# Turning two of four attention heads with VectorE and a trip through DRAM instead of TensorE

## The chip, the cores and the metric

The kernel runs on one core of a Trainium2 chip. A core has five engines that run their own instruction streams side by side and wait for each other by semaphores: TensorE (PE in the profile; PEld is its weight load) multiplies matrices into PSUM, VectorE (DVE) and ScalarE (ACT) work elementwise and along rows, GpSimd (POOL) helps, and SyncE (SP) here issues nearly all DMAs. The metric is the device time of one execution in microseconds. Before the change the median of three runs is 820.45 us (820.26 to 821.07).

## The reference

For 16 batches of 128 rows and 1024 columns: a layer norm, grouped-query cross attention to a context (32 query heads of size 32, 8 key/value heads, four query heads to a key head), a residual, a second layer norm, a product with a 0/1 matrix whose last fifth of the rows counts as -4, a scale and a second residual.

```python
Q = query @ Wq + bq
K = key @ Wk + bk
V = value @ Wv + bv
...
scores = jnp.einsum('bhgqd,bhkd->bhgqk', Q, K) * scale
w = jax.nn.softmax(scores, axis=-1)
y = jnp.einsum('bhgqk,bhkd->bhgqd', w, V)
...
x = x + _L0_xattn_ref(_layernorm(x, axis=-1), ctx_4096, ctx_4096, ...)
x = x + _L0_ffn_ref(_layernorm(x, axis=-1), L0_ffn_kernel, L0_ffn_scale)
```

## The kernel before, in words

All data are float32. The 16 batches go in eight **groups** of two (`grp` 0 to 7). The attention of a group falls into four **steps**: for each of the two chunks `a` of four key heads, the two batches. A step (`attend`, L669, then `weighted`, L551) works as follows.

- `scores` (L506): 16 groups of matmuls of 32 rows write, for each key head `i` of the chunk, a PSUM tile of 128 query positions by 4 query heads by 128 key positions.
- `exponentials` (L522), for each of the four key heads: VectorE takes the negative maximum (`negm`, L525), ScalarE writes `p`, the exponential, once for each query head with its sum (L529).
- `divide` (L538): VectorE takes the reciprocal (L540) and multiplies `p` in place (L541).
- `turn` (L543): TensorE transposes the four 128x128 blocks of `p` against the identity (`tpp`, L546), as the sum over key positions needs the key position in the partitions; ScalarE copies the result from PSUM to SBUF (`pt`, L548).
- `weighted` (L551): four matmuls of 512 columns with `v` as weights (`av`, L556), and a copy to `yT` (L564).

The score tiles, `p` and `pt` each have four buffers, one to a key head.

Between these the other work of the group is woven in: the query projection (`prep_q`, L430; matmuls at L396) and output projection (`out_proj`, L568; L607), each made of seven products instead of eight with sums of blocks (`seven`, L407) whose weights do not fit and are streamed from DRAM in **pieces** of 512 KB through a ring of eight (`fetch`, L213, issued on SP at L218), the key and value projections (`accumulate`, L293), and the second product (`ffn`, L652, also L293) with its transposes (`ffn_transpose`, L636). `norm_x` (L335) normalizes the next group's `x` on VectorE, and `prep_x` (L329) transposes it on TensorE (`tp_x`, L310). The next context is loaded by eight 128 KB DMAs a group, each to 32 partitions (`load_ctx`, L151, issued at L156); VectorE turns it in blocks of 32x32 (`turn_ctx`, L314, L319). The output is stored at L667.

The order is written out by hand by `Stream` (L23). It has a queue of generators, each of which emits a piece of TensorE work and yields its cost in microseconds, and a list of events with due times. `run` (L52) fires each event whose due time has passed, then emits the next piece and adds its cost to the clock. An event may add a cost too (0.45 for a `turn`). So an event lands at the first boundary between pieces after its due time; a piece of the output projection costs 2 x 512/600 = 1.71, one of the query projection 2 x 128/600 = 0.43. Instructions of each engine run in the order in which they are emitted here.

A step starts with the scores (1.2 on the clock). `first` for key head `i` is due 0.7 + 2.4 i after that, `divide` 2.3 after `first`, and the turn `length`/2 - 3.0 after `first` (L681 to L687). Other work is then emitted until `length` - 2.0 after the step's start (L872), in the last step of a group until the queue is empty (L870), and then until all four heads are turned (L873). Then comes `weighted`. `length` (L815) is 17.4 in group 0, 24.0 in groups 1 to 5 and 22.0 in group 6; group 7 has its own rule (L857 to L864).

Of the kernel before, what the change touches and what calls it, by code (L numbers as in the profile page):

```python
# [9 lines left out]
FP = mybir.dt.float32  # L10
# [7 lines left out]
P = 128  # L18
# [58 lines left out]
def once(fn, *args):  # L77
    fn(*args)
    yield 0.0
# [3 lines left out]
def kernel(  # L83
# [16 lines left out]
    nc = tc.nc  # L100
    B, S, D = x.shape
    KV = Wk.shape[1]
    F = ffn_w.shape[1]
    HD = 32
    NG = D // KV
    NI = P // HD
# [11 lines left out]
    const = ctx.enter_context(tc.tile_pool(name="const", bufs=1))  # L118
    dram = ctx.enter_context(tc.tile_pool(name="dram", bufs=1, space=bass.MemoryType.DRAM))
    work = ctx.enter_context(tc.tile_pool(name="work", bufs=1))  # L120
    small = ctx.enter_context(tc.tile_pool(name="small", bufs=4))
    ps_mm = ctx.enter_context(tc.tile_pool(name="ps_mm", bufs=2, space=PSUM))
    ps_tp = ctx.enter_context(tc.tile_pool(name="ps_tp", bufs=2, space=PSUM))
    ps_sc = ctx.enter_context(tc.tile_pool(name="ps_sc", bufs=4, space=PSUM))

    ident = const.tile([P, P], FP, name="ident")
# [214 lines left out]
    def prep_k(grp):  # L341
        kT = work.tile([P, NA, T], FP, tag="kT", name=f"kT{grp}", bufs=2)
        kTs[grp] = kT
        for a in range(NA):
            mm = ps_mm.tile([P, T], FP, tag="mm", name=f"k_{grp}_{a}")
            yield from accumulate(
                mm, [(wk_sb[:, c, a * P : (a + 1) * P], chunk(cTs, grp, c)) for c in range(NC)]
            )
            nc.scalar.activation(kT[:, a], mm, AF.Identity, bias=bkT[:, a : a + 1])
            yield 0.85  # L350
# [13 lines left out]
    S4 = [P, NG, S]  # L364
# [139 lines left out]
    yTs = {}  # L504

    def scores(b, a):  # L506
        grp, cols = b // GB, slice(b % GB * S, (b % GB + 1) * S)
        qT, kT = qTs[b, a], kTs[grp]
        tiles = [ps_sc.tile([P, NG, S], FP, tag="sc", name=f"sc_{b}_{a}_{i}") for i in range(NI)]
        for g in range(NG):  # L510
            for i in range(NI):
                rows = slice(i * HD, (i + 1) * HD)
                nc.tensor.matmul(  # L513
                    tiles[i][:, g],
                    lhsT=qT[rows, g],
                    rhs=kT[rows, a, cols],
                    start=True,
                    stop=True,
                )
        return tiles  # L520

    def exponentials(b, a, i, tile_):  # L522
        n = f"{b}_{a}_{i}"
        negm = small.tile([P, NG], FP, tag="negm", name=f"negm_{n}")
        nc.vector.tensor_reduce(negm, tile_, AX.X, ALU.max, negate=True)  # L525
        p = work.tile([P, NG, S], FP, tag="p", name=f"p_{n}", bufs=4)
        total = small.tile([P, NG], FP, tag="total", name=f"total_{n}")
        for g in range(NG):
            nc.scalar.activation(  # L529
                p[:, g],  # L530
                tile_[:, g],
                AF.Exp,
                bias=negm[:, g : g + 1],
                accum_out=total[:, g : g + 1],
            )
        return p, total

    def divide(b, a, i, p, total):  # L538
        inv = small.tile([P, NG], FP, tag="inv", name=f"inv_{b}_{a}_{i}")
        nc.vector.reciprocal(inv, total)  # L540
        nc.vector.tensor_mul(p, p, inv.unsqueeze(2).to_broadcast([P, NG, S]))  # L541

    def turn(b, a, i, p):  # L543
        tp = ps_tp.tile([P, NG, S], FP, tag="tp", name=f"tpp_{b}_{a}_{i}")
        for g in range(NG):
            nc.tensor.transpose(tp[:, g], p[:, g], ident)  # L546
        pt = work.tile([P, NG, S], FP, tag="pt", name=f"pt_{b}_{a}_{i}", bufs=4)
        nc.scalar.copy(pt, tp)  # L548
        return pt

    def weighted(b, a, pts):  # L551

        mm = ps_tp.tile([P, NG, S], FP, tag="tp", name=f"av_{b}_{a}")
        for i in range(NI):
            h = a * NI + i
            nc.tensor.matmul(  # L556
                mm[i * HD : (i + 1) * HD],
                lhsT=vs[b][:, h * HD : (h + 1) * HD],
                rhs=pts[i],
                start=True,  # L560
                stop=True,
            )
        yTs[b, a] = work.tile(S4, FP, tag="yT", name=f"yT{b}_{a}", bufs=7)
        nc.scalar.copy(yTs[b, a], mm)  # L564

    x2Ts, x2ns, x2stats = {}, {}, {}

# [98 lines left out]
        if b < B - 1:  # L666
            nc.sync.dma_start(out=out[b], in_=x_t)  # L667

    def attend(b, a, length):  # L669


        tiles = scores(b, a)
        stream.now += 1.2
        pts = [None] * NI
        for i in range(NI):

            def first(i=i):
                p, total = exponentials(b, a, i, tiles[i])
                stream.later(2.3, lambda: divide(b, a, i, p, total))

                def third():  # L681
                    pts[i] = turn(b, a, i, p)
                    return 0.45

                stream.later(length / 2 - 3.0, third)

            stream.later(0.7 + 2.4 * i, first)  # L687
        return pts

    def combine(w, k, part):  # L690

# [44 lines left out]
    NGRP = B // GB  # L736
    with tc.manual_schedule():
        stream = Stream()
# [15 lines left out]
        def plain(a):  # L754
            return prep_q_plain(a, {(r, k): at_q[r, a, k] for r in range(2) for k in range(2)})
# [47 lines left out]
        def between(gen, n, fn, *args):  # L803

            for i, us in enumerate(gen):
                yield us
                if i + 1 == n:
                    fn(*args)

        for grp in range(NGRP):  # L810
            b0, b1, nxt = grp * GB, grp * GB + 1, grp + 1
            p0, p1 = b0 - 2, b0 - 1
            first, more = grp == 0, nxt < NGRP
            last = grp == NGRP - 1
            length = 17.4 if first else 24.0 if grp < NGRP - 2 else 22.0  # L815
            if first:
                stream.add(
                    once(prep_ctx, nxt, 12.5, 13.5),
                    between(plain(1), 9, sums_of_wq, 0),
                    once(sums_of_wq, 1),  # L820
                    once(turn_ctx, nxt * GB, 1),
                    once(turn_ctx, nxt * GB + 1, 1),
                    once(norm_x, nxt * GB),
                    prep_k(nxt),
                    once(get_ctx, nxt + 1),
                    once(norm_x, nxt * GB + 1),
                    prep_v(nxt),
                    prep_x(nxt, 0),
                    prep_x(nxt, 1),
                    once(convert_ffn),  # L830
                    between(qs[nxt], 40, residuals, grp),
                )
            elif more:
                stream.add(
                    once(get_x, nxt * GB, 14.0),
                    once(prep_ctx, nxt, 3.7, 8.0, 13.0, 18.0),
                    os[grp - 1],
                    once(get_ctx, nxt + 1),
                    prep_k(nxt),
                    mixed(prep_v(nxt), chain(ffn_transpose(p0), ffn_transpose(p1)), 1, 2),  # L840
                    once(get_x, nxt * GB + 1, 5.0),
                )
                if nxt < NGRP - 1:
                    stream.add(ffn(p0), mixed(ffn(p1), prep_x(nxt, 0), 12))
                else:
                    stream.add(mixed(ffn(p0), prep_x(nxt, 0), 14))
                stream.add(once(residuals, grp), prep_x(nxt, 1), qs[nxt])
            else:
                stream.add(
                    os[grp - 1],  # L850
                    mixed(ffn(p1 - 2), ffn_transpose(p0), 10, 2),
                    once(load_residual, b0, 2.0),
                    mixed(ffn(p0), ffn_transpose(p1), 8, 2),
                    once(load_residual, b1, 2.0),
                )
            if not more:
                for q in range(2 * NA):  # L857
                    b, a = grp * GB + q % GB, q // GB
                    start = stream.now
                    pts = attend(b, a, 15.0)  # L860
                    stream.later(15.0, lambda b=b, a=a, pts=pts: weighted(b, a, pts) or 1.0)
                    stream.run(start + 12.0)
                stream.drain()
                break  # L864
            for q in range(2 * NA):
                b, a = grp * GB + q % GB, q // GB
                start = stream.now
                pts = attend(b, a, length)
                if q == 2 * NA - 1:
                    stream.run(start + length - 2.0, lambda: stream.queue)  # L870
                else:
                    stream.run(start + length - 2.0)  # L872
                stream.run(stream.now, lambda: None in pts)  # L873
                weighted(b, a, pts)
                stream.now += 1.0
        stream.add(
            os[NGRP - 1],
# [54 lines left out]
```

## Time and profile before

| what | value |
|---|---|
| median of three runs | 820.45 us |
| the profiled execution, and its span | 817.83 us, 816.1 us |
| one of groups 1 to 5 | 97.5 to 97.6 us |
| group 6, group 7 | 92.5 us, 110.8 us |
| transposes of `p` on TensorE (L546) | 512, mean 273 ns |
| copies of them on ScalarE (L548) | 128, mean 590 ns |
| block transposes of the context on VectorE (L319) | 32, mean 698 ns |
| pieces of weights | 218 DMAs of 512 KB, 4.4 to 4.8 us to land (medians by source) |
| DMA over the span | 165.14 MB, 202 GB/s |

The profile shows one execution. A group of instructions is named by its line in the kernel, its engine and what it writes and reads. A mean duration is that of one instruction from its start to its modelled end, and matmuls overlap; the chain of work that ended last gives each piece of work only the time by which it put off what came after. The span is the profiled time from first to last instruction. A DMA has an issue on SP's queue (SPq) and a landing. Where the text gives an instruction's time, it is from the span's start; where it gives a time within a step, it is from the step's first score matmul.

### The profile page before, as it was taken

The page shows a single profiled execution, that of the slowest core. Times are in us where ns is not written, and L with a number is a line of the kernel's source. Part 1 is how long each engine was busy: PE and PEld are TensorE (multiplying, and loading weights), DVE is VectorE, ACT ScalarE, POOL GpSimd, SP SyncE. Part 2 cuts the span into 40 slices and gives each one's busy share as a digit, 9 for nine tenths or more (in the row PEclk, how much of TensorE's full clock was granted, in tenths as well). Part 3 has the DMA queues.
Part 4 walks back from the last instruction along what each step waited for, and adds up shares of the span by engine and source line. Part 5 has one row for each costly group of instructions (what it writes and reads, how often), then busy time and mean ns, then how long its engine had stood idle before and what let it go on. Part 6 is the DMA issues. An engine that isn't in the chain of part 4 may idle for free.

```text
span 816.1 us, 13885 instructions
## 1 busy us (share of the span) xinstructions
PE 789.8 (97%) x5216; PEld 593.4 (73%) x5216; DVE 459.9 (56%) x862; ACT 332.7 (41%) x1281; POOL 69.6 (9%) x109
## 2 busy tenths in 40 slices
PE   3997999999999999999999999999999999999998
PEld 3886884678947797488965889568894779756556
DVE  1369748554475554755456454765348565467442
ACT  0243854444334443345333544344434454366200
POOL 1000003002000020000300002000200002000300
PEclk9999999999999999999999999999999999999999
DMA  9999598715885178741887328780578307761511
GB/s 202 357 319 317 198 399 326 210 52 182 273 269 164 43 238 274 262 130 44 286 269 253 80 103 280 276 242 29 179 262 281 132 27 274 246 215 69 195 62 77
DMA packets 81075, 165.14 MB, mean 202 GB/s; under 512 B 5969, under 2 KB 42833, under 8 KB 81009
## 3 DMA queue, kind: packets, MB, share of 16 engines
q1 hardware_dynamic: 79200, 162.55, 59.6%
q10 hardware_dynamic: 1664, 1.57, 1.1%
q8 instruction: 41, 0.67, 0.3%
q0 software_dynamic: 144, 0.14, 0.1%
q14 instruction: 26, 0.20, 0.1%
HBM read 147.46 MB, written 16.78 MB: 201 GB/s over the span
## 4 chain that ended last, share of the span: by engine, by line
PE 86%; DMA 6%; DVE 3%; issue 2%; SPq 1%; ACT 1%; POOL 0%; ACTq 0%; DVEq 0%; POOLq 0%
PE o_u L607 14%; PE f L293 14%; PE q_u L396 12%; PE o_v L607 7%; PE tpp L546 6%; PE q_v L396 6%; PE k L293 5%; PE v L293 5%; PE sc L513 4%; PE av L556 4%; PE o_c L607 3%; PE q_c L396 3%; DMA wo<-in_L_xattn_Wo_dram 2%; PE tp_f L646 2%; PE tp_x L310 1%
## 5 line engine op out<-in xcount | busy, mean ns | idle before, releaser
L529 ACT ACTIVATE p<-sc,negm 128x128 f32<-128x128 f32 x512 | 181.1, 369 | 155.9 <-DVE negm L525 82.3
L548 ACT COPY pt<-tpp 128x512 f32<-128x512 f32 x128 | 74.8, 590 | 117.1 <-PE tpp L546 116.6
L525 DVE TENSOR_REDUCE negm<-sc 128x4 f32<-128x512 f32 x128 | 87.3, 683 | 39.8 <-PE sc L513 39.8
L293 PE MATMUL f<-wf_sb,x2l 128*128 128x512 f32 x256 | 106.0, 414 | 0.0
L529 ACT ACTIVATION_READ_ACCUMULATOR p<-sc,negm 128x1 f32 x512 | 105.8, 207 | 0.0
L293 PE MATMUL f<-wf_sb,x2h 128*128 128x512 f32 x256 | 101.2, 396 | 0.0
L541 DVE TENSOR_TENSOR p<-p,inv 128x512 f32<-128x512 f32 x128 | 88.6, 692 | 4.4
L546 PE MATMUL tpp<-ident,p 128*128 128x128 f32 x512 | 76.7, 273 | 6.3 <-DVE p L541 4.0
L546 PEld LDWEIGHTS tpp<-ident,p 128*128 128x128 f32 x512 | 61.7, 141 | 28.1 <-issue 20.0
L396 PE MATMUL q_u<-t,piece 128*128 128x128 f32 x672 | 81.2, 276 | 0.0
L396 PEld LDWEIGHTS q_u<-t,piece 128*128 128x128 f32 x672 | 78.0, 192 | 0.2 <-DMA piece<-q 0.2
L293 PE MATMUL v<-wv_sb,cT 128*128 128x256 f32 x256 | 62.6, 387 | 12.3 <-DMA wv_sb<-in_L_xattn_Wv_dram 12.3
L178 POOL TENSOR_TENSOR x<-x,bo_b 128x256 f32<-128x256 f32 x64 | 48.8, 795 | 180.2 <-DMA x<-in_x_dram 160.1
L293 PEld LDWEIGHTS v<-wv_sb,cT 128*128 128x128 f32 x256 | 47.5, 195 | 17.7 <-issue 12.3
L607 PE MATMUL o_u<-piece,yT 128*128 128x512 f32 x128 | 59.1, 603 | 0.0
L607 PE MATMUL o_u<-piece,s 128*128 128x512 f32 x128 | 59.0, 594 | 0.0
L607 PE MATMUL o_v<-piece,s 128*128 128x512 f32 x128 | 59.0, 594 | 0.0
L293 PE MATMUL k<-cT,wk_sb 128*128 128x256 f32 x256 | 57.0, 380 | 0.0
L293 PEld LDWEIGHTS f<-wf_sb,x2l 128*128 128x128 f32 x256 | 48.1, 188 | 11.4 <-issue 1.1
L293 PEld LDWEIGHTS f<-wf_sb,x2h 128*128 128x128 f32 x256 | 48.3, 189 | 10.0 <-issue 0.5
L293 PEld LDWEIGHTS k<-cT,wk_sb 128*128 128x128 f32 x256 | 48.5, 190 | 9.0 <-issue 2.6
L564 ACT COPY yT<-av 128x512 f32<-128x512 f32 x32 | 18.7, 585 | 88.0 <-PE av L556 88.0
(77 smaller groups left out, 949.8 us busy)
## 6 DMA issues: line engine op xcount, KB each, us to landing
piece<-o SPq DMA_DIRECT2D x64, 512.0 KB, 4.4
piece<-q SPq DMA_DIRECT2D x56, 512.0 KB, 4.4
piece<-in_L_xattn_Wq_dram SPq DMA_DIRECT2D x50, 512.0 KB, 4.8
piece<-in_L_xattn_Wo_dram SPq DMA_DIRECT2D x48, 512.0 KB, 4.5
xn<-in_x_dram SPq DMA_DIRECT2D x16, 512.0 KB, 5.4
x<-in_x_dram SPq DMA_DIRECT2D x16, 512.0 KB, 4.9
ctx<-in_ctx_dram SPq DMA_DIRECT2D x60, 128.0 KB, 5.9
out_dram<-x SPq DMA_DIRECT2D x15, 512.0 KB, 2.7
```

Source lines behind the costliest of these rows:

```text
L178: lambda cut=cut: nc.gpsimd.tensor_add(x_t[:, cut], x_t[:, cut], bo_b[:, cut]) and None,
L293: nc.tensor.matmul(mm, lhsT=lhsT, rhs=rhs, start=k == 0, stop=k == n - 1)
L396: nc.tensor.matmul(mm if part is None else mm[:, part], lhsT=lhsT, rhs=rhs, start=start and n == k == 0, stop=k == len(some) - 1, skip_gro ...
L513: nc.tensor.matmul(tiles[i][:, g], lhsT=qT[rows, g], rhs=kT[rows, a, cols], start=True, stop=True,)
L525: nc.vector.tensor_reduce(negm, tile_, AX.X, ALU.max, negate=True)
L529: nc.scalar.activation(p[:, g], tile_[:, g], AF.Exp, bias=negm[:, g : g + 1], accum_out=total[:, g : g + 1],)
L541: nc.vector.tensor_mul(p, p, inv.unsqueeze(2).to_broadcast([P, NG, S]))
L546: nc.tensor.transpose(tp[:, g], p[:, g], ident)
L548: nc.scalar.copy(pt, tp)
L556: nc.tensor.matmul(mm[i * HD : (i + 1) * HD], lhsT=vs[b][:, h * HD : (h + 1) * HD], rhs=pts[i], start=True, stop=True,)
L564: nc.scalar.copy(yTs[b, a], mm)
L607: nc.tensor.matmul(mm, lhsT=lhsT[:, 2 * k + c], rhs=w[:, c], start=start and k == c == 0, stop=k == c == 1, skip_group_check=True,)
```

## The change

In groups 1 to 6, the first two of a step's four key heads are no longer transposed by TensorE. VectorE transposes their scaled `p` in place, in blocks of 32x32 (`turn_blocks`). What is left is to move whole blocks between quarters of the partitions: SP stores both heads to DRAM in one DMA (`store_blocks`), and fetches them back in four DMAs of 128 KB, one to each quarter of 32 partitions (`fetch_blocks`). For this the exponentials of the two heads are written in blocks of 32 key positions, the two heads side by side, so that a block row of both is 1 KB. `p` and `pt` become two constant tiles of four heads each, `p_all` and `pT_all`, in place of four rotating buffers each. The turned `p` of all heads lies with the query block outermost, and the weighted sum reads four runs of 128 columns and is put in order by the copy to `yT`. The other two heads, and all heads of groups 0 and 7, go through TensorE as before. The division and the turn of a block-turned head are one event, due 2.3 after its exponentials; the store is due 3.0 after that of head 1, the fetch 4.5 after the store. `weighted` still stands at the end of its own step. `length` becomes 23.2 in groups 1 to 5 and 21.2 in group 6.

```diff
+    NK, NP = S // HD, NI // 2
+    p_all = const.tile([P, NI, NG * S], FP, name="p_all")
+    pT_all = const.tile([P, NP, NK, 2, NG * HD], FP, name="pT_all")
+    p_dram = dram.tile([NP, NK, P, 2 * NG * HD], FP, name="p_dram")
+
+    def probabilities(i, blocks):
+        if blocks:
+            pair = p_all[:, i - i % 2 : i - i % 2 + 2].rearrange("p i n -> p (i n)")
+            pair = pair.rearrange("p (t i g k) -> p i g t k", t=NK, i=2, g=NG)
+            return pair[:, i % 2]
+        return p_all[:, i].rearrange("p (g t k) -> p g t k", t=NK, g=NG)
...
-                p[:, g],
-                tile_[:, g],
+                p[:, g],
+                tile_[:, g].rearrange("p (t k) -> p t k", t=NK),
...
+        if blocks:
+            p = probabilities(i, blocks).rearrange("p g t k -> p t g k")
+            factor = inv.unsqueeze(1).unsqueeze(3).to_broadcast([P, NK, NG, HD])
+        else:
+            p = p_all[:, i].rearrange("p (g s) -> p g s", g=NG)
+            factor = inv.unsqueeze(2).to_broadcast(S4)
+        nc.vector.tensor_mul(p, p, factor)
...
-        pt = work.tile([P, NG, S], FP, tag="pt", name=f"pt_{b}_{a}_{i}", bufs=4)
-        nc.scalar.copy(pt, tp)
-        return pt
+        nc.scalar.copy(
+            pT_all[:, i // 2, :, i % 2].rearrange("p k (g q) -> p g k q", g=NG),
+            tp.rearrange("p g (k q) -> p g k q", k=NK),
+        )
+
+    def turn_blocks(i):
+        p = probabilities(i, True).rearrange("p g t k -> p t g k")
+        nc.vector.transpose(p, p)
+
+    def store_blocks(pair):
+        p = p_all[:, 2 * pair : 2 * pair + 2].rearrange("p i n -> p (i n)")
+        nc.sync.dma_start(
+            out=p_dram[pair].rearrange("t p n -> p t n"),
+            in_=p.rearrange("p (t n) -> p t n", t=NK),
+        )
+        stream.later(4.5, lambda: fetch_blocks(pair))
+
+    def fetch_blocks(pair):
+        for t in range(NK):
+            nc.sync.dma_start(
+                out=pT_all[t * HD : (t + 1) * HD, pair].rearrange("r k i n -> r k (i n)"),
+                in_=p_dram[pair, t].rearrange("(k r) n -> r k n", r=HD),
+            )
...
-                rhs=pts[i],
+                rhs=pT_all[:, i // 2, :, i % 2],
...
-        nc.scalar.copy(yTs[b, a], mm)
+        nc.scalar.copy(
+            yTs[b, a].rearrange("p g (k q) -> p k g q", k=NK), mm.rearrange("p k g q -> p k g q")
+        )
...
-    def attend(b, a, length):
+    def attend(b, a, length, via_dram=False):
...
+                blocks = via_dram and i < 2
+                total = exponentials(b, a, i, tiles[i], blocks)
+
+                def by_tensor():
+                    turn(b, a, i)
+                    pending.discard(i)
                     return 0.45
+
+                def by_vector():
+                    divide(b, a, i, total, blocks)
+                    turn_blocks(i)
+                    pending.discard(i)
+                    if i == 1:
+                        stream.later(3.0, lambda: store_blocks(0))
+
+                if blocks:
+                    stream.later(2.3, by_vector)
+                else:
+                    stream.later(2.3, lambda: divide(b, a, i, total, blocks))
+                    stream.later(length / 2 - 3.0, by_tensor)
...
-            length = 17.4 if first else 24.0 if grp < NGRP - 2 else 22.0
+            length = 17.4 if first else 23.2 if grp < NGRP - 2 else 21.2
...
-                pts = attend(b, a, length)
+                pending = attend(b, a, length, not first)
...
-                stream.run(stream.now, lambda: None in pts)
-                weighted(b, a, pts)
+                stream.run(stream.now, lambda: pending)
+                weighted(b, a)
```

More of the change, by code (lines that the diff above doesn't have):

```diff
@@ L520, in scores, with exponentials @@
         return tiles
-    def exponentials(b, a, i, tile_):
+    NK, NP = S // HD, NI // 2
[8 more added lines that the diff above has]
+        return p_all[:, i].rearrange("p (g t k) -> p g t k", t=NK, g=NG)
+    def exponentials(b, a, i, tile_, blocks):
+        p = probabilities(i, blocks)
         n = f"{b}_{a}_{i}"
@@ L525, in exponentials @@
         nc.vector.tensor_reduce(negm, tile_, AX.X, ALU.max, negate=True)
-        p = work.tile([P, NG, S], FP, tag="p", name=f"p_{n}", bufs=4)
         total = small.tile([P, NG], FP, tag="total", name=f"total_{n}")
@@ L535, in exponentials, with divide, turn, weighted @@
             )
-        return p, total
-    def divide(b, a, i, p, total):
+        return total
+    def divide(b, a, i, total, blocks):
         inv = small.tile([P, NG], FP, tag="inv", name=f"inv_{b}_{a}_{i}")
         nc.vector.reciprocal(inv, total)
-        nc.vector.tensor_mul(p, p, inv.unsqueeze(2).to_broadcast([P, NG, S]))
-    def turn(b, a, i, p):
+        if blocks:
[5 more added lines that the diff above has]
+        nc.vector.tensor_mul(p, p, factor)
+    def turn(b, a, i):
         tp = ps_tp.tile([P, NG, S], FP, tag="tp", name=f"tpp_{b}_{a}_{i}")
         for g in range(NG):
-            nc.tensor.transpose(tp[:, g], p[:, g], ident)
-        pt = work.tile([P, NG, S], FP, tag="pt", name=f"pt_{b}_{a}_{i}", bufs=4)
-        nc.scalar.copy(pt, tp)
-        return pt
-    def weighted(b, a, pts):
-        mm = ps_tp.tile([P, NG, S], FP, tag="tp", name=f"av_{b}_{a}")
+            nc.tensor.transpose(tp[:, g], p_all[:, i, g * S : (g + 1) * S], ident)
+        nc.scalar.copy(
[18 more added lines that the diff above has]
+            )
+    def weighted(b, a):
+        mm = ps_tp.tile([P, NK, NG, HD], FP, tag="tp", name=f"av_{b}_{a}")
         for i in range(NI):
@@ L667, in ffn @@
             nc.sync.dma_start(out=out[b], in_=x_t)
-    def attend(b, a, length):
+    def attend(b, a, length, via_dram=False):
         tiles = scores(b, a)
         stream.now += 1.2
-        pts = [None] * NI
+        pending = set(range(NI))
         for i in range(NI):
             def first(i=i):
[L678 to L682, printed above, removed]
-                    return 0.45
-                stream.later(length / 2 - 3.0, third)
+                blocks = via_dram and i < 2
[3 more added lines that the diff above has]
+                    pending.discard(i)
+                    return 0.45
+                def by_vector():
[9 more added lines that the diff above has]
+                    stream.later(length / 2 - 3.0, by_tensor)
             stream.later(0.7 + 2.4 * i, first)
-        return pts
+        return pending
     def combine(w, k, part):
@@ L859 @@
                     start = stream.now
-                    pts = attend(b, a, 15.0)
-                    stream.later(15.0, lambda b=b, a=a, pts=pts: weighted(b, a, pts) or 1.0)
+                    attend(b, a, 15.0)
+                    stream.later(15.0, lambda b=b, a=a: weighted(b, a) or 1.0)
                     stream.run(start + 12.0)
```

## The prediction

> **What bounds the kernel now.** I read the page first: busy shares, then the chain of work that ended last.
>
> ```profile
> PE 789.8 (97%) x5216; PEld 593.4 (73%) x5216; DVE 459.9 (56%) x862; ACT 332.7 (41%) x1281; POOL 69.6 (9%) x109
> ...
> PE 86%; DMA 6%; DVE 3%; issue 2%; SPq 1%; ACT 1%; POOL 0%; ACTq 0%; DVEq 0%; POOLq 0%
> ```
>
> TensorE is busy nearly always and holds 86% of the chain. Since the change touches groups 1 to 6 only, I then asked for busy time by stretch. The columns are length, then busy time of PE, PEld, DVE, ACT and POOL, PEclk, DMA share and GB/s. The first row is group 3, the second group 6, the third the first step of group 3 and the fourth its last.
>
> ```profile
> 320.00:417.60 97.60, 97.60 (x669) 74.24 (x665) 55.20 (x104) 40.53 (x158) 8.32 (x12) 1.00 0.60 195
> 612.70:705.20 92.50, 90.67 (x633) 68.17 (x633) 53.43 (x103) 39.84 (x158) 7.74 (x12) 1.00 0.56 188
> ...
> 319.00:343.60 24.60, 24.60 (x108) 11.70 (x108) 18.02 (x33) 8.94 (x37) 0.55 (x1) 1.00 0.84 279
> 391.80:416.50 24.70, 24.70 (x248) 23.58 (x244) 10.46 (x19) 8.85 (x37) 5.42 (x8) 1.00 0.81 269
> ```
>
> In group 3 (and 1, 2, 4, 5, all 97.5 to 97.6 long) PE never waits: each microsecond of PE work removed there is gained, until something else is late. Group 6 already has 1.83 us of PE waits. In a group's first and last step DMA is busy 0.84 and 0.81 of the time.
>
> **What is removed from PE.** The chain in time (start, us, what) through group 3's first step:
>
> ```profile
> 330.57 1.72 PE o_v L607 x4
> 332.29 0.44 PE tpp L546 x4
> 332.73 1.72 PE o_v L607 x4
> ...
> 342.63 0.99 PE av L556 x8
> 343.62 1.10 PE sc L513 x32
> ```
>
> A head's four transposes hold PE for 0.44 us, although the page gives each 273 ns: durations overlap. Over the window 320 to 420 sixteen such runs hold 7.0% of 100 us, 0.4375 each. Two heads a step, four steps, six groups: 48 x 0.4375 = **21.0 us removed**. [...] ACT also loses 48 copies of 590 ns; ACT is off the path and this is worth nothing.
>
> **What is added to DVE.** 48 block transposes. The nearest row does the same operation on the same 128x512 f32:
>
> ```profile
> L319 DVE STREAM_TRANSPOSE cT<-ctx 128x512 f32<-128x512 f32 x32 | 22.0, 698 | 13.4 <-DMA ctx<-in_ctx_dram 13.4
> ```
>
> 0.70 us each, 0.61 from start to start in a back-to-back run (negm at 347.92, x at 348.52). That is 5.6 us more in 94 for an engine busy 55 of 97.6. It hides behind PE in groups 1 to 5, as nothing on PE waits there now; if that cover went, each step would lose up to its 1.2 us, 24 us over 20 steps. I take nothing. In group 6 the cover is gone, as the chain shows:
>
> ```profile
> 667.12 0.69 DVE p L541
> 667.82 1.21 DVE st_a L276 x2
> 669.02 0.03 issue
> ...
> 670.17 0.81 DVE xn L285
> 670.98 0.10 DVE inv L540
> 671.08 0.05 issue
> 671.13 0.64 PE tp_x L310 x4
> ```
>
> From 656.2 to 671.1 the chain alternates between ACT and DVE, and PE waits for the normalized xn. PE work before it shrinks by six runs, 2.6 us; but the chain's start moves by only four runs (1.75), and two block transposes stand in it (+1.2). So 0.55 is gained in place of 2.6: **2.1 given back**.
>
> The exponentials, the scaling and the copies are written in 32-element pieces, and the weighted sum reads four pieces of 128. The block transposes of ctx already write such pieces at 698 ns against 692 for a plain pass. 128-wide matmuls cost 3.57/32/128 = 0.87 ns a column against 3.43/8/512 = 0.84 for 512-wide ones: 0 to 4% of 0.99 us on 32 sums, at most 1.3. I take nothing.
>
> **The new wait: the weighted sum on the fetch.** A step now has one store of 512 KB and four fetches of 128 KB on SP. Behind the store (which waits for DVE) and the fetch (which waits for the store's landing) stand the weight pieces. The ring of eight covers them: 8 x 1.72 us of PE work less 4.5 to land leaves 9.3. So the pieces hold, and what can be late is the fetch itself; behind the sum on PE stands the next step's score matmuls, for which DVE's negm and all that follows wait. Rows for it:
>
> ```profile
> L156 SPq DMA_DIRECT2D ctx<-in_ctx_dram x60: 311/422/592, 0.7 to 548.9; - x60
> ...
> DMA to landing us min/median/max: 3.0/5.9/12.6
> ```
>
> ctx has the fetch's very shape: 32 partitions, 128 KB. Four issues take 3 x 0.42 = 1.3 us to the last. One lands 3.0 us later when the queues are quiet, and up to 6.6 in the bursts of eight in the middle groups. So from first issue to last landing, **L lies between 4.3 and 7.9**. The pieces in these stretches land 4.5 after issue (median), which gives 1.3 + 4.5 = 5.8; I add 0.5, since the first step's DMA has 0.84 x 24.6 = 20.7 us of work at 332 GB/s busy rate, and 1.05 MB more needs 3.2: about 23.9 in a step of 23.7. L = 6.3.
>
> The store: head 1's division ends 8.4 to 8.9 us after the first score matmul today, so its block transpose ends by 10.1, ahead of the store's place (10.4 to 11.5). No row shows 1 KB packets written to DRAM; 512 KB writes land in 2.7 (out_dram) to 6.2 us (o<-wo). I take 4.5, between them, as pieces do: it lands just as the fetch is due; 6.2 would add 0.7 to the waits of first steps. The next step's exponentials overwrite p_all 24 us after, long past this.
>
> When is the fetch issued? The planner fires events only between pieces of 1.71 us in the first step: at 1.2 + 1.71k after the first score matmul. Tried on today's kernel: its first turn is due at 11.9, so falls to 13.2; the step begins at 318.97, and tpp at 332.29 is 13.3. After the change: head 1's exponentials 4.6, its division and turn 8.05, store 11.5, fetch 16.6. SP issues a piece first: 17.0. The sum is placed at 1.2 + 12 x 1.71 + 2 x 0.45 = 22.7 (today's rule gives 23.6; the row says 23.7). It waits 17.0 + 6.3 - 22.7 = 0.6 us. Ends: L 4.3 no wait, 7.9 2.2.
>
> In group 6 the length is 21.2, so the sum comes after ten pieces, at 19.3 (today 20.2 by rule and row), while the fetch keeps its delays: 17.0 + 6.3 - 19.3 = 4.0 us (2.0 to 5.6). Last step: pieces of 0.43, fetch 15.5, sum about 22.5: 7.0 of room, no wait (0.9 at 7.9). Second and third step: no piece stands on SP there, so the fetch goes when the store has landed, at about 16 (behind ctx) and 13.5; sums at 21.7 and 22.5 or later: no wait. Group 6's third step: SP stands at L667 for the output until 672.5, so the fetch may come late: 0.5 (0 to 1.5).
>
> [...]
>
> **The sum.** -21.0 + 2.1 + 5 x 0.6 + 4.0 + 0.5 = -11.4. The profiled execution took 817.83 (span 816.1) and becomes 806.4; the median of the runs, 820.45, 2.6 above it, becomes **809.0**.
>
> **Rivals.**
> - *In time everywhere.* L at 4.3 leaves 2.0 in group 6 and no other wait: -21.0 + 2.1 + 2.0 = -16.9, 803.6; all gained is 799.5. For it: DMA is quiet in second and third steps. Against: 0.84 in the first.
> - *Late by more in the first and last steps.* L = 7.0: 5 x 1.3 + 4.7 + 2.6 = 13.8 back, 813.2; to 818.8.
> - *Slower: the fetch is later than the work it replaces.* One mechanism, at L556: PE stands for blocks behind saturated queues. With waits of L - 5.7 in five first steps, L - 7.0 in five last ones and L - 2.3 in group 6, plus 2.6, it decides from L = 7.65. L = 9 gives 35.8 - 21.0 = +14.8, 835. For it: ctx bursts land 7.2 to 8.0 after their first issue for the fourth of eight. Against: those had eight in flight, not four.
> - *The change doesn't do what it says*: PE's tpp runs stay; the diff leaves no such path, so no chance of its own.
>
> **Chances.** Forecast (804.5 to 813) 0.46; in time 0.20; late by more (813 to 818.8) 0.12; within 0.2%, about what a measurement of this kernel can tell from no change (818.8 to 822.1), 0.06; slower 0.16. So faster 0.46 + 0.20 + 0.12 = 0.78. Leaving out the slower and no-change cases nearly whole, and the last of the in-time one, the range is 801 to 818.
>
> **What would show it.** tpp falls from 512 to 320 matmuls; PE busy falls by about 21; DVE gains 48 stream transposes of 0.7. In each group's first step PE waits under 1 us before the weighted sum for the fetch, in group 6's first step about 4, and before tp_x there about 3.7 in all. Wrong if PE waits for the fetch in second or third steps, if pieces are late, or if DVE releases PE in groups 1 to 5.

## The result, and the profile after

The change made the kernel slower: 855.17 us (median), a ratio of 1.0412 to before (95% interval 1.0374 to 1.0450). I had forecast 809.0 in a range of 801 to 818. The profiled execution took 856.9 us; its span is 855.1, which is 39.0 more than before. One of the four executions (866.27 us) was in a slower state and is left out of the ratio.

From the page after: busy times, the granted clock in 40 slices (the line of before stands ahead of that of after), and the chain by engine.

```profile
PE 789.2 (92%) x5024; PEld 584.6 (68%) x5024; DVE 490.2 (57%) x910; ACT 307.7 (36%) x1233; POOL 69.5 (8%) x109
...
PEclk9999999999999999999999999999999999999999
PEclk9999999899999999899998999989999898999999
...
PE 63%; DMA 24%; DVE 5%; SPq 4%; issue 3%; ACT 1%; POOL 0%; ACTq 0%; POOLq 0%; DVEq 0%
```

PE has 192 matmuls fewer and yet is not less busy. DMA now holds 24% of the chain, where it held 6%, and the clock, whole in every slice before, dips about once a group. Who waits:

```profile
PE av L600 <- DMA pT_all<-p_dram: 38.2, 13, 6.2
PE v L293 <- DMA wv_sb<-in_L_xattn_Wv_dram: 12.2, 1, 12.2
PE tpp L570 <- DVE p_all L564: 4.0, 2, 3.4
PE tp_x L310 <- DVE xn L285: 3.1, 1, 3.1
```

The weighted sum waits for the fetch 13 times, 38.2 us in all; the list has no PE wait for a weight piece (the wait for `wv_sb` is the first load of the kernel, 12.3 before). The chain through group 3's first step, which starts at 331.05:

```profile
339.29 3.45 PE o_u L653 x8
...
343.20 6.60 DMA p_dram<-p_all
...
349.81 0.33 SPq L590
350.14 0.05 issue
350.20 0.43 SPq L590
...
351.14 6.89 DMA pT_all<-p_dram
358.03 0.20 issue
358.23 1.94 PE av L600 x8
360.17 2.02 PE sc L513 x32
```

The store goes out at 12.1 us of the step, behind two pieces on SP and 0.6 after the 11.5 that I had worked out, and needs 6.6 us to land. Only then does the first fetch go (18.8), and the last has landed at 27.0. PE had reached the sum at 22.9 and stood 4.3 us. And then the sum takes 1.94 us in place of 0.99, and the scores 2.02 in place of 1.10. Busy time and clock in three stretches, the five after the restart, the four after that, and five in the middle of the fetch (columns as in the prediction):

```profile
358.20:363.10 4.90, 4.87 (x42) 2.55 (x43) 0.89 (x2) 0.70 (x2) 0.00 (x0) 0.51 0.45 174
363.10:367.00 3.90, 3.90 (x13) 2.12 (x12) 2.89 (x7) 2.22 (x13) 0.55 (x1) 1.00 0.37 121
...
352.00:357.00 5.00, 1.96 (x5) 0.57 (x3) 1.53 (x3) 0.00 (x0) 0.00 (x0) 0.92 1.13 195
```

After the wait PE runs at half clock (0.51) until 363.1. The profile's clock has one stretch of 6.8 us at half speed here, which begins within the wait, at 356.2; I call such a stretch a **half-clock window**. In the middle of the fetch the DMA engines are full (1.13 by overlapping packets) but move only 195 GB/s.

Where the 39.0 us come from, by the trace (a half-clock window, at a granted clock of 0.50, costs half of the PE work that falls in it; group 3's sum took 1.94 us there for 0.99):

| part | us |
|---|---|
| transposes gone from PE, 48 x 0.4375 | -21.0 |
| waits for the fetch in the six first steps (4.4, 6.2, 4.3, 4.5, 5.8, 5.6) | +30.8 |
| half clock after them (windows of 6.8 us) | +13.3 |
| waits in the six last steps (0.3 to 1.3) | +4.5 |
| group 6's third step: wait 2.9; longer wait at tp_x 1.2; two half-clock windows 3.1 | +7.2 |
| group 0 is longer; 1.7 of it is a half-clock window after a wait of 3.4 us that before has too, without the window | +2.1 |
| sum | 36.9 |

2.1 us are not placed. The kernel without the dependency, below, has a like amount: its groups 1 to 5 are shorter by 3.0 us each and not by the 3.5 of the transposes.

### The profile page after: what moved, and what is told of

Its sections match the earlier page's. It is cut to its first block, busy times and chain, and to the rows that moved or that the text cites. A ratio compares the mean times of both kernels' runs of the same rounds, so it can differ in the third digit from the quotient of the medians.

```text
span 855.1 us, 13629 instructions
## 1 busy us (share of the span) xinstructions
PE 789.2 (92%) x5024; PEld 584.6 (68%) x5024; DVE 490.2 (57%) x910; ACT 307.7 (36%) x1233; POOL 69.5 (8%) x109
## 4 chain that ended last, share of the span: by engine, by line
PE 63%; DMA 24%; DVE 5%; SPq 4%; issue 3%; ACT 1%; POOL 0%; ACTq 0%; POOLq 0%; DVEq 0%
PE f L293 13%; PE o_u L653 11%; DMA pT_all<-p_dram 10%; DMA p_dram<-p_all 9%; PE v L293 5%; PE k L293 5%; PE av L600 5%; PE q_u L396 5%; PE sc L513 5%; PE o_c L653 3%; PE q_c L396 3%; PE tpp L570 2%; PE o_v L653 2%; SPq L590 2%; PE tp_f L692 2%
## 5 line engine op out<-in xcount | busy, mean ns | idle before, releaser
L546 ACT ACTIVATE p_all<-sc,negm 128x128 f32<-128x128 f32 x512 | 181.1, 367 | 187.1 <-DVE negm L543 91.1
L546 ACT ACTIVATION_READ_ACCUMULATOR p_all<-sc,negm 128x1 f32 x512 | 105.0, 205 | 0.0
L564 DVE TENSOR_TENSOR p_all<-p_all,inv 128x512 f32<-128x512 f32 x128 | 89.3, 697 | 4.4
L571 ACT COPY pT_all<-tpp 128x512 f32<-128x512 f32 x80 | 46.4, 590 | 99.9 <-PE tpp L570 99.6
L600 PE MATMUL av<-pT_all,v 128*32 128x512 f32 x256 | 41.8, 689 | 38.2 <-DMA pT_all<-p_dram 38.2
L293 PE MATMUL v<-wv_sb,cT 128*128 128x256 f32 x256 | 65.5, 400 | 12.2 <-DMA wv_sb<-in_L_xattn_Wv_dram 12.2
L293 PEld LDWEIGHTS v<-wv_sb,cT 128*128 128x128 f32 x256 | 49.3, 202 | 18.5 <-issue 12.2
L513 PEld LDWEIGHTS sc<-kT,qT 32*128 32x128 f32 x1024 | 37.0, 215 | 30.6 <-issue 30.6
```

The source lines that it names most:

```text
L293: nc.tensor.matmul(mm, lhsT=lhsT, rhs=rhs, start=k == 0, stop=k == n - 1)
L513: nc.tensor.matmul(tiles[i][:, g], lhsT=qT[rows, g], rhs=kT[rows, a, cols], start=True, stop=True,)
L546: nc.scalar.activation(p[:, g], tile_[:, g].rearrange("p (t k) -> p t k", t=NK), AF.Exp, bias=negm[:, g : g + 1], accum_out=total[:, g : g ...
L564: nc.vector.tensor_mul(p, p, factor)
L571: nc.scalar.copy(pT_all[:, i // 2, :, i % 2].rearrange("p k (g q) -> p g k q", g=NG), tp.rearrange("p g (k q) -> p g k q", k=NK),)
L600: nc.tensor.matmul(mm[i * HD : (i + 1) * HD], lhsT=vs[b][:, h * HD : (h + 1) * HD], rhs=pT_all[:, i // 2, :, i % 2], start=True, stop=True,)
```

## The experiments

**Theory.** The loss is one wait, in steps in which weight pieces already fill DMA: store and fetch land late there, and PE's long idle stretch lowers its clock. **Rivals**: the added traffic or VectorE's added work costs by itself; the quarter transfers are slow wherever they stand; the plan issues them too late.

**No dependency on the fetch.**

```diff
-                rhs=pT_all[:, i // 2, :, i % 2],
+                rhs=pT_all[:, 1, :, i % 2],
```

> As the change, with store and fetch as they are, but the weighted sum of all four heads reads the two heads that TensorE turned, so that nothing on PE waits for the fetch; the output of two heads in four is not the reference's. Theory (the loss is the wait and what follows from it): no wait before the sum, clock 1.0 throughout, and nearly all of the 21.0 us of transposes gained: 801 to 804. Rival (the added traffic costs by itself, by late weight pieces or a busier VectorE): PE waits for pieces or DVE, 810 or more.

Measured: 802.13 us, ratio 0.9783 (0.9747 to 0.9820). Group 3 in this kernel:

```profile
312.50:407.01 94.51, 94.27 (x637) 70.85 (x633) 60.41 (x112) 36.27 (x150) 8.20 (x12) 1.00 0.78 247
```

94.5 us in place of 97.5, full clock, no wait for pieces, although DMA is busy 0.78. So the traffic and VectorE's turns are nearly free in groups 1 to 5 (0.5 us a group), and the loss is the wait and what follows from it. PE's wait at tp_x in group 6 is 3.1 here too, so that one is VectorE's and not the fetch's.

**Half the weight traffic.**

```diff
+            c = src.shape[1]
+            some = c if n < RING else c // 2
-            nc.sync.dma_start(out=t.rearrange("p (c n) -> p c n", c=src.shape[1]), in_=src)
+            nc.sync.dma_start(out=t.rearrange("p (c n) -> p c n", c=c)[:, :some], in_=src[:, :some])
```

> As the change, but of each weight piece after the first eight only half the columns' blocks are loaded, and the matmuls read that half twice: same PE work, half the weight traffic; the output is not the reference's. Theory (the store and the fetch are late because they queue behind the pieces): in first steps the store lands in about 4 us, the fetch in about 4.5 from its first issue, as they do in second and third steps today (3.7 and 4.2); no wait before the sum, 801 to 804. Rival (a fetch to quarters of the partitions is slow in itself): fetch still 8 us in first steps, waits of 3 us or more, 840 or more.

Measured: 805.56 us, ratio 0.9825 (0.9778 to 0.9871). In first steps the store lands in 3.9 us and the fetch in about 5.0 (once 5.7); five of six sums wait 0.3 us or less, group 6's waits 1.3. A little above the forecast; the theory's mechanism holds: the pieces in the queue make both transfers late.

**One fetch of 128 partitions.**

```diff
-        for t in range(NK):
-            nc.sync.dma_start(
-                out=pT_all[t * HD : (t + 1) * HD, pair].rearrange("r k i n -> r k (i n)"),
-                in_=p_dram[pair, t].rearrange("(k r) n -> r k n", r=HD),
-            )
+        nc.sync.dma_start(
+            out=pT_all[:, pair].rearrange("p k i n -> p k (i n)"),
+            in_=p_dram[pair].rearrange("t p n -> p t n"),
+        )
```

> The four fetches of 32 partitions each become one of 128 partitions with the same 512 packets of 1 KB; blocks land in the wrong quarters, so the output is not the reference's. It separates the form of the fetch from the queue it stands in. If the queue alone is at fault: first issue to landing in first steps stays at 6.5 us or more, waits of 2 us or more, time 830 to 845. If the form is most of it: it falls to about 5 us as for a piece, the wait in first steps to under 1 us, and the time to 805 to 812.

Measured: 822.46 us, ratio 1.0046 (1.0024 to 1.0067), between the two forecasts. The stretch of the fetch in group 3's first step, after the change and here, and the wait here:

```profile
350.00:358.00 8.00, 3.96 (x13) 1.69 (x11) 3.29 (x5) 1.07 (x2) 0.20 (x1) 0.89 1.12 255
...
338.10:343.90 5.80, 4.19 (x15) 1.93 (x13) 3.30 (x5) 1.07 (x2) 0.45 (x1) 1.00 1.07 355
...
PE av L599 <- DMA pT_all<-p_dram: 15.7, 7, 3.5
```

In group 3's first step the fetch takes 5.8 us in place of 8.2; while it runs, the engines, full in both, now move 355 GB/s in place of 255. The wait shrinks to 1.8 to 2.3 us (3.5 in group 6). So neither rival alone: the quarter form costs 2.4 us and more where DMA is full, while in quiet steps it costs little (4.2 against 3.7 us). Up to 1.3 us of this is the time that SP takes to issue the other three fetches (0.42 us each, the median of the 96 at L590 after the change). What makes up the rest no run here shows.

**The quarters on the store's side.** This version computes what the change computes: four stores of 32 partitions, then one fetch in 4 KB packets.

```diff
-        nc.sync.dma_start(
-            out=p_dram[pair].rearrange("t p n -> p t n"),
-            in_=p.rearrange("p (t n) -> p t n", t=NK),
-        )
+        for k in range(NK):
+            nc.sync.dma_start(
+                out=p_dram[pair, :, :, k].rearrange("t r n -> r t n"),
+                in_=p[k * HD : (k + 1) * HD].rearrange("r (t n) -> r t n", t=NK),
+            )
...
+        nc.sync.dma_start(
+            out=pT_all[:, pair].rearrange("p k i n -> p k (i n)"),
+            in_=p_dram[pair].rearrange("t r k n -> (t r) (k n)"),
+        )
```

> The quarters go to the store's side: four stores of 32 partitions each, 1 KB packets, and then one fetch of 128 partitions in 4 KB packets; the result is the same. If the form of the quarter transfers is what makes the fetch slow, the fetch now lands within about 5 us of its issue, but the store takes 2 us longer: issue 20 to 21, landing 25 to 26, wait 2 to 3 us, mostly without half clock, 825 to 838. If the queue alone counts, the sum of store and fetch stays as it is (15.4 us from the store's issue to the last landing in first steps) and the time at 850 to 860.

Measured: 824.98 us, ratio 1.0079 (1.0049 to 1.0109). Waits of 1.5 to 2.5 us in first steps, 3.7 in group 6. The fetch takes 6.2 us in group 3, and the stores land 6.2 to 6.7 us after their first issue, as the single store did (6.1 to 6.6): the 2 us that I expected them to lose did not come. During them the engines move 323 GB/s in group 3, during the single store 320. So the quarter form costs less in the store, which reads SBUF, than in the fetch, which writes it; why is open. The size of the packets is not what made the fetch slow: 4 KB packets here take no less than the 1 KB packets of the whole fetch (5.8 us).

**The store earlier.**

```diff
-                        stream.later(3.0, lambda: store_blocks(0))
+                        stream.later(0.3, lambda: store_blocks(0))
```

> The store is due 0.3 after head 1's block transpose in place of 3.0; nothing else changes. Theory (queue and form of the transfers set the landing): in first steps the store goes out at about 9.9 in place of 12.1, still takes about 6 us, and the fetch about 8.5 from there: landing near 25, waits of 1.5 to 3 us, half clock in few of them: 828 to 838. Rival (the plan's delays are the cause): the sum finds its blocks there, waits under 0.5 us, 805 to 810.

Measured: 830.64 us, ratio 1.0141 (1.0106 to 1.0175), as the theory expected: the store goes out 1.7 us sooner in first steps, the waits are 1.9 to 3.4 us and 5.1 in group 6. All but one of the six draw a half-clock window, where I had expected few. The plan's delay is a part of the wait, and not its cause. Quarter stores and the early store together:

> The sum in its own step, the quarters on the store's side with one fetch, and the stores due 0.3 after head 1's block transpose. With quarter stores alone the sum waited 1.5 to 2.5 us in first steps (3.7 in group 6) and the time was 825.0. If the remaining wait is only lateness of issue, 2.2 us earlier takes it to under 0.5 us (1.5 in group 6): 804 to 810, faster than before. If the earlier store only queues longer behind the pieces, 818 or more.

Measured: 812.61 us, ratio 0.9921 (0.9890 to 0.9951), faster than before and 2.6 above the forecast. First steps wait 0.2 to 1.2 us; group 6's waits 2.9 and draws a half-clock window of 6.8 us.

**Work for PE while it waits.**

```diff
+        for n in range(warm):
+            c = n % (NC // 2) * 2
+            nc.tensor.matmul(
+                mm.rearrange("p k g q -> p (k g q)"),
+                lhsT=ident,
+                rhs=wk_sb[:, c : c + 2].rearrange("p c n -> p (c n)"),
+                start=True,
+                stop=True,
+            )
...
-                weighted(b, a)
+                weighted(b, a, 5 if q == 0 and not first else 0)
```

> As the change, with five matmuls of 512 columns against the identity (0.86 us each, 4.3 us; their result is overwritten) ahead of the weighted sum in the first steps, so that PE works while it waits. Theory (an idle gap over about 3 us halves the granted clock for 3.4 to 6.8 us): the waits shrink from 4.3-6.2 to under 2 us, the half-clock windows after first steps vanish, and the time falls by the 13.3 us of work that was run at half clock there: about 842. Rival (the half clock has another cause, such as the load before it): windows stay, time 855 or more.

Measured: 847.30 us, ratio 1.0334 (1.0295 to 1.0373). The same point of group 3, and the waits:

```profile
349.30 7.85 DMA pT_all<-p_dram
357.15 0.09 issue
357.24 1.07 PE av L609 x8
358.31 1.10 PE sc L513 x32
...
PE av L609 <- DMA pT_all<-p_dram: 17.0, 10, 2.5
```

The fetch is as late as before, but PE now waits 2.4 us at most in first steps, the sum takes 1.07 us and the scores 1.10 again: no half-clock window follows a first step (granted clock 1.00 from 353.5 to 362 here, 0.51 from 358.2 to 363.1 after the change). So it was the idle time, and not the load before it, that lowered the clock in these steps. The 3 us of the theory were no limit here: a gap of 2.9 us drew half clock after the change, one of 3.36 us before it did not (last section). The time falls by 8 and not by 13, because the waits in last steps grow from 4.5 to 10.2 us: their fetches take 7.1 to 9.1 us in place of 4.9 to 7.7. Why they do is open.

**The first step given back to TensorE.**

```diff
-                pending = attend(b, a, length, not first)
+                pending = attend(b, a, length, not first and q > 0)
```

> The first step of each of groups 1 to 6 goes back to TensorE for all four heads; the other three steps stay as changed. Theory (the first step is where the cost sits: its DMA queue is full, the fetch lands late, PE stands 4.3 to 6.2 us and then runs on at half clock): the six waits (30.8 us) and the half-clock work after them (13.3 us) go, six times 0.875 us of transposes come back: 855.2 - 44.1 + 5.3 = about 816. Rival (the wait is the fetch's own slowness and every step pays it alike): the other steps' waits stay or grow and the time stays above 840.

Measured: 826.63 us, ratio 1.0101 (1.0063 to 1.0139). The first steps' waits go as expected, but the forecast missed by 10. Waits in later steps:

```profile
PE av L600 <- DMA pT_all<-p_dram: 7.4, 10, 1.6
...
PE f L293 <- DVE x L706: 5.4, 5, 1.1
PE tp_x L310 <- DVE inv L557: 3.4, 1, 3.4
```

The waits for the fetch, 7.4 us, are no more than the other steps had after the change (38.2 less 30.8). New is a wait for VectorE: the first step's sum now starts at 21.9 (22.9 after the change), more work is left for the third and fourth step, and in the third VectorE's chain comes onto PE's path, 1.1 us a group; only the kernels with the late sum, below, have that wait too, of 0.3 us. These 5.4 us, and 1.7 in group 6's waits for VectorE and in half-clock windows, place some 7 of the 10; the rest is open.

**ScalarE's queue.** `nc.scalar.dma_start` in place of `nc.sync.dma_start` for store and fetch.

> Store and fetches are issued from ScalarE's queue in place of SyncE's, at the same places of the plan. If they are late because they stand in line behind the pieces on SyncE's queue, then in a queue of their own they land sooner: store in about 4.5, fetch in about 6 from its first issue in first steps, waits of 0 to 1.5 us, 808 to 818. If the shared DMA engines are full whoever issues, landing times stay (6.3 and 8 to 10 us) and so does the time, with ScalarE standing up to 2 us for the store's landing on top: 855 or more.

Measured: 908.13 us, ratio 1.1095 (1.1066 to 1.1123).

```profile
p_dram<-p_all ACTq DMA_DIRECT2D x24, 512.0 KB, 4.7
pT_all<-p_dram ACTq DMA_DIRECT2D x96, 128.0 KB, 6.1
...
PE av L600 <- DMA pT_all<-p_dram: 74.1, 13, 7.0
```

Worse: fetches take 9.7 to 11.1 us in first steps of groups 1 to 5 and 8.7 to 10.1 in last steps, where they took 8.2 to 10.7 and 4.9 to 7.7 after the change. Each of the 13 waits, 4.6 to 7.0 us, draws a half-clock window of 6.8. The stores of first steps land in 5.6 to 6.3 us, hardly sooner than from SP. So the time behind pieces in the same line was not the trouble, which fits engines that are full whoever issues. Why the fetch gets even slower stays open.

**The lengths alone**, in the kernel before:

> The kernel before with the changed step lengths alone (23.2 and 21.2 in place of 24.0 and 22.0). PE's work and its order of magnitude stay, and PE never waited in groups 1 to 5, so the time should stay within 0.3% of before, 818 to 821; a rival is that the lengths themselves move work onto VectorE's path in group 6, 822 or more.

Measured: 818.84 us, ratio 1.0002 (0.9990 to 1.0014): no part of the loss.

**The sum in the next step.**

```diff
-                weighted(b, a)
-                stream.now += 1.0
+                if not first and q < 2 * NA - 1:
+                    stream.later(7.0, lambda b=b, a=a: weighted(b, a) or 1.0)
+                else:
+                    weighted(b, a)
+                    stream.now += 1.0
```

and the second and third step run until `length` - 1.0.

> The weighted sum of the first three steps of groups 1 to 6 is moved 7 us into the next step (some 30 us after its own step's start); the last step's stays. Transfers and turns are the change's. Theory (the loss is only the wait for blocks that land 27 to 29 us after the first step's start): the first steps' waits and the half clock go, what stays are 0.3 to 1.3 us in last steps and group 6's normalization: 802 to 808, faster than before by 1.5% or more. Rival (a full DMA queue makes something else late instead: weight pieces, or the last step's fetch by more): 812 or more, with PE waits at the projections or 3 us or more in last steps.

Measured: 806.15 us, ratio 0.9856 (0.9827 to 0.9885). The stretch around the end of group 3's first step:

```profile
334.58 3.43 PE o_v L653 x8
338.01 1.10 PE sc L513 x32
339.12 3.63 PE o_u L653 x8
342.75 2.59 PE k L293 x12
345.34 0.99 PE av L600 x8
346.33 4.52 PE k L293 x20
...
PE av L600 <- DMA pT_all<-p_dram: 2.1, 2, 1.5
```

The fetch of that step still takes 9.3 us, but the sum stands after scores and projections of the next step, 1.9 us behind the last landing, and PE does not stop. With the quarter stores on top:

> Both cures: the sums of the first three steps 7 us into the next step, and the quarters on the store's side with one fetch. If the late sum already hides all but the last steps, the faster fetch takes away only what is left there and in group 6 (0.6 + 1.5 us): 803 to 806, at most 2 us under the late sum alone. If something of the transfers still costs PE elsewhere, the time stays at 806 or more.

Measured: 805.62 us, ratio 0.9845 (0.9809 to 0.9881). It has no wait for the fetch over 0.3 us left; from the late sum alone it can't be told apart. Both beat the kernel before and the change.

## Why the prediction was wrong, point by point

- **21.0 us removed from PE**: right in kind. With the wait taken away, group 3 falls by 3.0 us of the 3.5, and the kernel by 2.2%.
- **VectorE's turns, 0.70 each, hidden in groups 1 to 5**: right. The 48 turns take 712 ns each, and none shows as a PE wait there. In group 6 I gave PE 3.7 us of waits before tp_x; it had 3.1.

```profile
L578 DVE STREAM_TRANSPOSE p_all<-p_all 128x512 f32<-128x512 f32 x48 | 34.2, 712 | 1.6
```

- **The ring covers the pieces**: right; no PE wait for a piece in any step.
- **"At 4.5 it lands just as the fetch is due"**: the first step that failed. The store went out at 12.1 in place of 11.5 and took 6.1 to 6.6 us in first steps, the upper row that I had named (6.2) and left. The fetch went at 18.3 to 18.8 in place of 17.0.
- **"L = 6.3"**: the term that failed by most. It was 8.2 to 10.7 in first steps, beyond my upper end of 7.9. I had worked out 23.9 us of DMA work for a step of 23.7 and charged 0.5 us for it. With no time to spare there, the pieces and the quarter form together cost 2 to 4 us more than that: with half the pieces' bytes L was 4.9 to 5.7, and as one transfer among all the pieces 5.8 to 6.0, either of them under my 6.3. A row had told it: ctx bursts, of the same form, took 7.2 to 8.0 to the fourth landing, and I set them aside because eight were in flight. Where DMA was quiet, L was 4.0 to 4.7, about my lower end of 4.3.
- **Waits by step**: second and third steps without a wait in groups 1 to 5, right; last steps 0.3 to 1.3 where I had none (in groups 1 to 5 the store took 5.7 to 6.6 and L was 6.7 to 7.7); group 6's first 5.6 for 4.0, its third 2.9 for 0.5, since the fetch did stand behind the output on SP (issued at 19.7).
- **The rival that came true** is "the fetch is later than the work it replaces". Its rule gives 835 at L = 9, and the mean L of first steps was 9.1; I gave it 0.16. What it lacked, and I nowhere had, is the **clock**: after such waits PE ran on at half speed (granted clock 0.51 in group 3), which cost 13.3 us after first steps and 3.1 later in group 6. I put the clock at nothing, as no row of before showed a clock under 1.00 within the work, where PE's longest gap after its start was 3.36 us, in group 0; my own forecast had one of 4.0 us in group 6. After the change all nine gaps of 2.9 us and more from 60 us on drew half clock, and whole-fetch shows it after one of 2.1 us (last section).

## What to carry to other kernels

- Before moving work from a saturated engine into transfers, add their DMA time to the DMA work of the very step: near or over the step's length, take landing times from the fullest bursts with everything queued, not from medians.
- A wait on the engine that bounds the kernel cost its length here and, for gaps from 2.1 us on (whole fetch), often work at half the granted clock after it; filling gaps of 4.3 to 6.2 us, with the data as late, brought 855.17 down to 847.30 us.
- When a round trip can't be made shorter, put its consumer later: the same transfers, with the sum 7 us on, were worth -1.4% and not +4.1%.

## What the runs showed of the hardware that I had not expected

The half clock came in windows of 3.4 or 6.8 us. After the change, from 60 us on and within the work, they begin at 83.13, 151.40, 253.79, 356.19, 458.59, 560.99, 663.39, 704.35 and 718.01: 20, then five times 30, then 12 and 4 times 3.41 us apart, whatever the length of the gaps. Cut into stretches of 3.41 us at these points, the trace has nine at full clock in which PE was idle for 2.24 to 3.41 us, and each was followed by one at half clock; the two with 1.0 to 2.0 us of idle time (1.06 and 1.09) were not. A second stretch at half clock followed the six in which PE was idle for 1.38 to 3.37 us of the first, and none followed the three with 0.00 to 0.58. Two gaps of the whole-fetch kernel, in such stretches (columns as in the prediction; the clock is the third number from the end):

```profile
147.32:150.73 3.41, 1.32 (x13) 0.33 (x16) 0.69 (x1) 0.00 (x0) 0.00 (x0) 1.00 1.07 360
150.73:154.15 3.42, 3.42 (x34) 2.39 (x35) 1.50 (x3) 1.38 (x6) 0.00 (x0) 0.50 0.34 135
...
632.01:635.42 3.41, 1.67 (x4) 0.38 (x2) 2.28 (x4) 0.57 (x1) 0.00 (x0) 1.00 1.08 349
635.42:638.84 3.42, 1.62 (x28) 0.81 (x32) 0.00 (x0) 0.47 (x1) 0.00 (x0) 1.00 0.79 278
638.84:642.25 3.41, 3.41 (x27) 1.79 (x24) 1.57 (x3) 1.62 (x9) 0.00 (x0) 1.00 0.02 7
```

The gap of 2.1 us lies in one stretch, and the next one runs at half clock; the gap of 3.5 us is split between two (1.74 and 1.80 us idle), and no window follows. After the change each of the six gaps of 4.28 to 6.22 us drew 6.83 us, and with a shorter one it differed: of the early-store kernel's five gaps of 1.9 to 3.4 us four drew a window, and one of 2.5 us in the keep-busy kernel drew none. The gap of 3.36 us in group 0, in stretches counted back from the one window of before (817.46, behind the last instruction), is split before the change (1.55 and 1.81 us) and drew none; after it, it falls 0.86 and 2.50 us, and the window at 83.13 follows. Why the clock falls in such stretches no run here shows. A window of 3.41 us at a clock of 0.50 is worth up to 1.7 us, so single runs can differ by that.
